# A convolution chain's last stage: resident rows loaded ahead of the raw coefficients, and scaled five pieces later

## The chip, the cores and the metric

The kernel runs on one core of a Trainium2 chip. The metric is the device time of one launch in microseconds (us). Before the change three runs took 2479.8, 2480.79 and 2481.91 us; the median is 2480.79.

## The reference

Four layers are applied in turn to x of shape (4, 64, 256, 256), all in float32:

```python
def conv(x, ...):                      # layers 0, 2 and 3
    k = einsum('ijk,imk->ijmk', hx, hy)[0].transpose(2, 0, 1)  # rank-one filters from two small sine networks
    y = irfft2(rfft2(x, s=(512, 512)) * rfft2(k, s=(512, 512)) / 512, s=(512, 512))[..., :256, :256]
    return y + x * bias[:, None, None]
def haar(x, v, conv_w, tau):           # layer 1
    f1 = haar2d(x)                     # Haar transform of each image
    for i in range(2):
        f4 = einsum('bchw,oc->bohw', f1 * v[i], conv_w[i])
        acc += sign(f4) * relu(abs(f4) - tau[i])               # soft threshold
    return haar2d(acc, inverse=True) + x
x = conv(x, L0); x = haar(x, L1); x = conv(x, L2); x = conv(x, L3)
```

A filter is the product of a row filter and a column filter, so a convolution becomes matmuls with one triangular Toeplitz matrix for the rows and one for the columns. The multiplication by v commutes with the sum over channels, so the kernel applies it after the channel matmul.

## The kernel before, in words

The work is cut into 64 tiles t: two groups of two images, 32 rounds a group, four images of 256 x 256 to a tile (128 x 2048 floats). Phase A (`phase_a`) runs layer 0 and the forward transform, phase B (`phase_b`) mixes the channels and thresholds, phase C (`phase_c`) makes the inverse transform and layers 2 and 3. Phases pass data through DRAM tensors: `coef` (A to B), `mixed` and `unshrunk` (B to C). For the second group, phase B leaves the threshold of its second filter undone: it writes the raw coefficients to `unshrunk`, and phase C thresholds them. That is the step called `shrink`.

The order of the instructions is written out by hand: every engine runs its own list in the order in which the Python code emits it. A phase is a list of pieces. A round of phase C has 18 pieces, j = 0 to 17, in `piece(t, j)`. TensorE does in one round:

- j 0 to 3: rows of layer 2 for tile t (`c1r`), in two pairs of pieces
- j 4: first half of the inverse transform's matmul for tile t+1 (`c0ps`, L352)
- j 5 to 8: columns of layer 3 for tile t-2 (`c2c`)
- j 9 to 12: rows of layer 3 for tile t-1 (`c2r`)
- j 13: second half of `c0ps`
- j 14 to 17: columns of layer 2 for tile t (`c1c`)

Each pair of pieces, and each half of `c0ps`, takes one pair of PSUM banks from `banks()`, ten pairs a round. Three pairs of banks are used in turn, so a new one can be written only when the pair asked for three places earlier has been copied out. Copies out are put off with `later()` and emitted by `flush()` at the start of the next piece: ScalarE copies `c1r` and `c2r` to `ch` (L913) and `c0ps` to `z` (L901); VectorE adds the bias term to `c2c` and `c1c` (L932, to `o` and `cy`).

Beside this, GpSimd does the inverse transform's additions along the rows (L429) two tiles ahead, after ScalarE has scaled the loaded tile `g` (L406, seven multiplications). From round 29 on (t = `alone` - `AHEAD` = 32 - 3), shrink works three tiles ahead, for tile 32 and later. For each half of a tile it has five operations: x = raw * v into PSUM (VectorE, L845), its sign (ScalarE, L847), its absolute value (ScalarE, L849), minus the threshold (VectorE, L851), and the last product (VectorE, L854). GpSimd then adds the result to `g` (L880). `SHRINK` holds the pieces in which these ten operations are emitted. Both v and the threshold come from one resident tile `rows`, loaded once (L821, two DMAs of 512 KB) from `in_v_rows` and scaled in place by `scale_rows` with 14 ScalarE multiplications (L406).

All DMAs are issued by SyncE (SP). Eight semaphores are used in turn for them, so a DMA is issued only after the one eight places earlier has landed. A `raw` tile takes four DMAs of 256 KB (L816), a `g` tile four of 256 KB (L810), a Toeplitz pair four of 112 KB (L163), a `mixed` or `unshrunk` store one of 512 KB (L721, L729). The SBUF pool `late`, which holds `rows`, `raw` and `shrunk`, is opened where phase B's pool is closed, just ahead of round 29. In that round the emission is: j 0 loads raw 32, then rows; j 1 loads g 32; j 2 loads the filters of tile 30, and `scale_rows`; j 3 to 17 shrink 32, shifted by two pieces; j 5 loads raw 33.

Of the kernel before, what the change touches and what calls it, by code (L numbers as in the profile page):

```python
# [51 lines left out]
BLOCKS = N // ROW  # L52
# [28 lines left out]
C_PIECES = 4 * BLOCKS + 2  # L81
AHEAD = 3
SHRINK = (1, 2, 3, 5, 6, 10, 11, 12, 14, 15)
W = 2 * N

PAIR = 2 * 2 * ROUNDS * NB * W + NB * W

# [13 lines left out]
def conv_haar_kernel(  # L101
# [10 lines left out]
    def coefficients(name):  # L112
        return dram.tile([CI, STEPS // 2, PAIR], F32, tag=name, name=name)
# [3 lines left out]
    unshrunk = coefficients("unshrunk")  # L117
    thresholds = dram.tile([STEPS, 2, SHARED, 2 * W + PAD], F32, tag="thresholds", name="thresholds")
    filt = [dram.tile([ROUNDS, 2, REPEATS, ITEMS, PERIOD], F32, tag=f"filt{l}", name=f"filt{l}") for l in range(NL)]
# [176 lines left out]
    def half(r):  # L296
        return slice(r * ROW, (r + 1) * ROW)
# [13 lines left out]

    tau_sb = mp.tile([P, 2, W], F32, tag="tau", name="tau_sb")
    per_level_sb = mp.tile([P, N], F32, tag="per_level", name="per_level_sb")
# [11 lines left out]
    def put_thresholds(copies):  # L325

        n = copies.stop - copies.start
        of = tau_sb.rearrange("p i w -> p (i w)").unsqueeze(1).to_broadcast([P, n, 2 * W])
        nc.sync.dma_start(thresholds.rearrange("s r c w -> (s r) c w")[:, copies, : 2 * W], of)

# [111 lines left out]
    def flush():  # L442
        ops = list(waiting)
        waiting.clear()
        for op in ops:
            op()
# [5 lines left out]
    def all_rows(grp_tile, r, images, joined):  # L452

        parts = images.rearrange("(m q) (h n) k -> q m h (n k)", q=2, h=2)
        n = NB * W
        pairs = []
        for q in range(2):
            for h in (slice(0, 2),) if joined else (slice(0, 1), slice(1, 2)):
                at = grp_tile.offset + ((h.start * 2 + q) * ROUNDS + r) * n
                rows = [[PAIR, P // 2], [2 * ROUNDS * n, h.stop - h.start], [1, n]]  # L460
                pairs.append((bass.AP(grp_tile.tensor, at, rows), parts[q][:, h]))
        return pairs
# [329 lines left out]
    def phase_c():  # L792
# [7 lines left out]
        def load(t, k=slice(0, 4)):  # L800
            if t >= total:
                return
            if t < 2:
                g = bp.tile([P, 2, 2, W], F32, tag="v", name=f"g_{t}", bufs=3)
                st[t]["g"] = g.rearrange("p i k w -> p (i k w)").rearrange("p (n k) -> p n k", k=N)
            elif k.start == 0:
                st[t]["g"] = big("in", f"g_{t}", 3)
                st[t]["scales"] = scales(st[t]["g"])
            for rows, g in all_rows(mixed[t // ROUNDS], t % ROUNDS, st[t]["g"], False)[k]:
                nc.sync.dma_start(g, rows)  # L810

        def load_raw(t):
            if alone <= t < total:
                r = st[t]["raw"] = late["sb"].tile([P, 2 * M, N], F32, tag="raw", name=f"raw_{t}", bufs=2)
                for rows, to in all_rows(unshrunk, t % ROUNDS, r, False):
                    nc.sync.dma_start(to, rows)  # L816

        def load_rows():
            late["rows"] = late["sb"].tile([P, 2, 2, W], F32, tag="rows", name="rows")
            for r in range(2):  # L820
                nc.sync.dma_start(late["rows"][half(r)].rearrange("p k s w -> p (k s w)"), v_rows)  # L821

        def scale_rows():
            for k in range(2):
                for op in scales(late["rows"][:, k].rearrange("p s (h k) -> p (s h) k", h=2), (1.0, 0.5)[k]):
                    pass

        def shrink(t, k):

            if not alone <= t < total:  # L830
                return
            s = st[t]

            def split(name, h):
                return s[name].rearrange("p (s b h) k -> p s b (h k)", s=2, b=NB)[:, h]

            def rows(k, h):
                return late["rows"][:, k, h].unsqueeze(1).to_broadcast([P, NB, W])

            h, op = divmod(SHRINK.index(k), 5) if k in SHRINK else (0, -1)  # L840
            if op == 0:
                if h == 0:
                    s["shrunk"] = late["sb"].tile([P, 2 * M, N], F32, tag="shrunk", name=f"shrunk_{t}", bufs=2)
                s["x"] = late["ps"].tile([P, NB, W], F32, tag="x", name=f"x_{t}_{h}")
                nc.vector.tensor_tensor(s["x"], split("raw", h), rows(0, h), ALU.mult)  # L845
            elif op == 1:
                nc.scalar.activation(split("shrunk", h), s["x"], AF.Sign)  # L847
            elif op == 2:
                nc.scalar.activation(s["x"], s["x"], AF.Abs)  # L849
            elif op == 3:  # L850
                nc.vector.tensor_tensor(s["x"], s["x"], rows(1, h), ALU.subtract)  # L851
            elif op == 4:
                to = split("shrunk", h)
                nc.vector.scalar_tensor_tensor(to, s["x"], 0.0, to, ALU.max, ALU.mult)  # L854

        def scaled(t, count):
            if count and 1 < t < total:
                run(st[t]["scales"], count)

        def filters(t, l):  # L860
            if t < total:
                st[t]["toep", l] = load_toeplitz(l, t)
# [11 lines left out]
        def sums(t):  # L874
            if t < total:
                s = st[t]
                if t >= alone:
                    for h in range(2):
                        to, of = (s[k].rearrange("p (s n) k -> p s (n k)", s=2)[:, h] for k in ("g", "shrunk"))
                        nc.gpsimd.tensor_tensor(to, to, of, ALU.add)  # L880
                s["ci"] = big("t1", f"ci_{t}", 2)
                s["ops"] = inverse_free(s["g"], s["ci"], f"i{t}_", nc.vector if t < 2 else nc.gpsimd, levels(t))
# [54 lines left out]
        def store(t):  # L937
            if t < total - 1:
                n = 2 * CI if t < alone else CI
                for k in range(0, 2 * M, n):  # L940
                    stores.append(lambda k=k, y=st[t]["y"]: nc.sync.dma_start(out[t // ROUNDS, t % ROUNDS][:, k : k + n], y[:, k : k + n]))
            st[t].clear()
            for put in stores[: len(stores) if t >= alone else 1]:
                put()
            del stores[: len(stores) if t >= alone else 1]
# [3 lines left out]
        def piece(t, j):  # L949
            flush()  # L950
            if j == 0:
                sums(t + 2)
            if t >= alone - AHEAD:
                if j == 1:
                    load(t + 3)
            elif t == 0:
                pass
            elif j in (1, 3, 5, 7):
                load(t + 3, slice(j // 2, j // 2 + 1))
            if stores and j == C2 + BLOCKS + 3:  # L960
                stores.pop(0)()
            if j == 2:
                filters(t + 1, 1)
            if j == C2 + BLOCKS + 1 and t > 1:
                store(t - 2)
            if j == R2 + BLOCKS:
                filters(t, 2)
            first = t == alone - AHEAD
            if t >= alone - AHEAD:
                if j == 0 and first:  # L970
                    load_raw(alone)
                    load_rows()
                if j == 2 and first:
                    scale_rows()
                if j == BLOCKS + 1:
                    load_raw(t + AHEAD + 1)
                shrink(t + AHEAD, j - 2 * first)
            if R1 <= j < R1 + BLOCKS:
                if t < total:
                    rows(t, 1, j - R1)  # L980
            elif C2 <= j < C2 + BLOCKS:
                if 1 < t:
                    columns(t - 2, 2, j - C2)
            elif R2 <= j < R2 + BLOCKS:
                if 0 < t <= total:
                    rows(t - 1, 2, j - R2)
            elif j >= C1:
                if t < total:
                    columns(t, 1, j - C1)
            else:  # L990
                product(t + 1, int(j > BLOCKS))
            if t == 0:
                scaled(3, 2 * (2 * BLOCKS <= j < C1))
                scaled(2, int(j > 0))
            else:
                scaled(t + 3, {11: 3, 12: 2, 15: 1, 16: 1}.get(j, 0))
            if j > 0:
                step(t + 2, 1)
# [183 lines left out]
```

## Time and profile before

The profiled execution took 2491.59 us, of which its span is 2489.8 us; the median of the unprofiled runs is 2480.79 us.

| what | value |
|---|---|
| TensorE busy | 2261.5 us, 91% of the span |
| GpSimd busy | 2055.6 us, 83% |
| VectorE busy | 1792.3 us, 72% |
| ScalarE busy | 1392.0 us, 56% |
| moved by DMA | 688.03 MB, mean 276 GB/s |
| mean granted TensorE clock | 0.983 |

A profile's times are those of one execution, in us from the start of its span. "Busy" is the time in which an engine worked on an instruction; DMA issues and waits are not counted. A wait is named after what ended it. Rounds 29 and later begin near 1787 us and run to the end.

### The profile page before, as it was taken

The numbers are of one execution on the slowest core, as the hardware profiler recorded it, in microseconds if no ns is written. First come the engines' busy times: TensorE is split into PE (matmuls) and PEld (weight loads), VectorE is DVE, ScalarE is ACT, GpSimd is POOL, SyncE is SP. The second block draws the span as 40 slices with busy tenths as digits, with TensorE's granted clock in tenths as the row PEclk, the third lists the DMA queues.
The fourth block names the chain that finished last, engine by engine and source line by source line (L and its number), as shares of the span: only waits on it lengthen the run. The fifth ranks groups of instructions, "written<-read, shape, count | busy, mean of one in ns | idle before, by whom it ended". The sixth has DMA issues, their size and how long they took to land.

```text
span 2489.8 us, 119298 instructions
## 1 busy us (share of the span) xinstructions
PE 2261.5 (91%) x53298; PEld 1874.7 (75%) x53298; DVE 1792.3 (72%) x1959; ACT 1392.0 (56%) x2318; POOL 2055.6 (83%) x2412
## 2 busy tenths in 40 slices
PE   7999999777777777778999999999899999999999
PEld 5779897444444454556787887888789999999998
DVE  4533334999999999768777777777577777777763
ACT  2232233677777777255666666666555655565552
POOL 2988887899999999777777778777879999999990
PEclk9999999999999999888999999999999999999999
DMA  6778888899999999557999999999866666666643
GB/s 198 246 274 299 292 287 307 276 355 349 358 338 364 353 344 337 208 197 280 313 319 327 326 324 328 330 327 328 272 202 215 208 221 215 218 213 217 218 161 109
DMA packets 222969, 688.03 MB, mean 276 GB/s; under 512 B 31470, under 2 KB 32815, under 8 KB 218232
## 3 DMA queue, kind: packets, MB, share of 16 engines
q1 hardware_dynamic: 222456, 680.40, 78.5%
q8 instruction: 419, 6.86, 1.1%
q14 instruction: 94, 0.77, 0.1%
HBM read 428.16 MB, written 252.12 MB: 273 GB/s over the span
## 4 chain that ended last, share of the span: by engine, by line
PE 46%; DMA 4%; DVE 3%; issue 2%; SPq 1%; ACT 1%; DVEq 0%; ACTq 0%
PE c2r L340 10%; PE c2c L340 10%; PE c1c L340 9%; PE c1r L340 9%; PE c0ps L352 4%; PE f L653 3%; DMA g<-mixed 2%; DVE x L692 1%; DVE cy L932 1%; DMA toep<-filt 1%; SPq L163 1%; DVE x L672 0%; DMA raw<-in_v 0%; DMA unshrunk<-raw 0%; DVE m L697 0%
## 5 line engine op out<-in xcount | busy, mean ns | idle before, releaser
L429 POOL TENSOR_TENSOR i<-i,g 128x16 f32<-128x16 f32 x744 | 436.0, 606 | 27.2
L653 PE MATMUL f<-ft,mix 64*64 64x512 f32 x2048 | 304.2, 614 | 123.8 <-DVE x L672 108.0
L340 PEld LDWEIGHTS a2ps<-toep,ay 64*64 64x64 f32 x8192 | 303.6, 136 | 117.6 <-DVE f L521 52.7
L340 PE MATMUL a2ps<-toep,ay 64*64 64x192 f32 (+3 forms) x8192 | 337.1, 303 | 24.8 <-DVE f L521 20.5
L340 PEld LDWEIGHTS c2c<-toep,ch 64*64 64x64 f32 x8192 | 305.9, 135 | 55.5 <-ACT ch L913 14.8
L340 PEld LDWEIGHTS c1c<-toep,ch 64*64 64x64 f32 x8192 | 310.8, 133 | 42.6 <-issue 13.9
L340 PEld LDWEIGHTS a1ps<-toep,x 64*64 64x64 f32 x8192 | 285.5, 134 | 62.5 <-issue 39.3
L340 PE MATMUL c2c<-toep,ch 64*64 64x128 f32 (+3 forms) x8192 | 317.1, 299 | 11.9 <-ACT ch L913 10.0
L340 PE MATMUL c2r<-toep,cy 64*64 64x256 f32 (+3 forms) x8192 | 319.7, 298 | 5.1 <-issue 3.8
L340 PE MATMUL a1ps<-toep,x 64*64 64x256 f32 (+3 forms) x8192 | 315.4, 298 | 9.2 <-issue 5.3
L340 PEld LDWEIGHTS c2r<-toep,cy 64*64 64x64 f32 x8192 | 299.2, 134 | 32.2 <-issue 16.9
L340 PE MATMUL c1c<-toep,ch 64*64 64x128 f32 (+3 forms) x8192 | 317.6, 297 | 5.9 <-issue 4.9
L340 PE MATMUL c1r<-toep,z 64*64 64x256 f32 (+3 forms) x8192 | 314.5, 297 | 5.7 <-issue 3.7
L429 POOL TENSOR_TENSOR ci<-i,g 128x1024 f32<-128x1024 f32 x124 | 314.1, 2553 | 4.5
L340 PEld LDWEIGHTS c1r<-toep,z 64*64 64x64 f32 x8192 | 296.0, 133 | 28.7 <-issue 10.4
L715 POOL TENSOR_TENSOR gt<-m,ft 128x512 f32<-128x512 f32 x128 | 164.5, 1285 | 170.1 <-DVE m L697 150.9
L678 ACT ACTIVATE m<-x 128x1024 f32<-128x1024 f32 x194 | 205.9, 1061 | 165.8 <-DVE x L672 128.9
L488 ACT COPY ay<-a1ps 128x512 f32<-128x512 f32 x256 | 137.4, 589 | 275.7 <-PE a1ps L340 275.1
L913 ACT COPY ch<-c2r 128x512 f32<-128x512 f32 x256 | 137.4, 590 | 262.1 <-PE c2r L340 261.7
L672 DVE TENSOR_TENSOR x<-f,v 128x1024 f32<-128x1024 f32 x192 | 233.4, 1216 | 28.2 <-PE f L653 26.0
L508 DVE SCALAR_TENSOR_TENSOR x<-x,bias_sb,a2ps 128x512 f32<-128x512 f32 x256 | 179.5, 743 | 96.4 <-POOL f L390 48.4
L913 ACT COPY ch<-c1r 128x512 f32<-128x512 f32 x256 | 137.5, 594 | 164.5 <-PE c1r L340 164.1
(86 smaller groups left out, 3989.8 us busy)
## 6 DMA issues: line engine op xcount, KB each, us to landing
toep<-filt SPq DMA_DIRECT2D x768, 112.0 KB
ft<-coef SPq DMA_DIRECT2D x128, 512.0 KB
mixed<-gt SPq DMA_DIRECT2D x128, 512.0 KB
g<-mixed SPq DMA_DIRECT2D x256, 256.0 KB
x<-in_x SPq DMA_DIRECT2D x128, 256.0 KB
coef<-f SPq DMA_DIRECT2D x128, 256.0 KB
x<-in_x SPq DMA_DIRECT2D x32, 1024.0 KB
v<-in_v SPq DMA_DIRECT2D x64, 512.0 KB
```

Source lines behind the costliest of these rows:

```text
L163: nc.sync.dma_start(both[at : at + ROW // 2], src)
L340: nc.tensor.matmul(ps[r][half(c), j % 2, k * ROW :], data[half(r), c, k, bass.ts(j, ROW)], t(r, c)[:, : N - k * ROW], start=k == 0, stop=k ...
L352: nc.tensor.matmul(ps[r][half(c)].rearrange("p h k -> p (h k)"), matrix[half(r)], pairs(r, c).rearrange("p h k -> p (h k)"), start=True, s ...
L429: engine.tensor_tensor(to, s, d, op)
L488: later(lambda y=y, ps=ps: nc.scalar.copy(y, ps))
L508: nc.vector.scalar_tensor_tensor(to, old, bias_sb[:, c : c + 1], ps, ALU.mult, ALU.add)
L653: nc.tensor.matmul(un[u]["f4"][half(q), b, :], mixers[0][half(r), bass.ts(i, C)], st[s]["f"][half(r), b], start=True, stop=True, tile_posi ...
L672: nc.vector.tensor_tensor(un[u]["x"], un[u]["f4"], both(u, "v"), ALU.mult)
L678: nc.scalar.activation(un[u]["m"], un[u]["x"], AF.Sign)
L692: nc.vector.tensor_tensor(un[u]["a"], un[u]["a"], both(u, "tau"), ALU.subtract)
L715: nc.gpsimd.tensor_tensor(g[:, 0], m[:, 0], st[s]["f"][:, 0], ALU.add)
L913: later(lambda y=y, ps=ps: nc.scalar.copy(y, ps))
```

## The change

Only round 29 is touched, and in later rounds nothing of the emission. Rows are loaded at j 0 in place of raw 32; raw 32 at j 3; `scale_rows` is emitted at j 7, not 2; raw 33 at j 9, not 5; and shrink of tile 32 takes the ten pieces 8 to 17 in place of 3, 4, 5, 7, 8, 12, 13, 14, 16, 17. The arithmetic and the number of instructions are unchanged. Nothing in the diff touches phase B's parting step, which is on VectorE in both kernels.

```diff
 SHRINK = (1, 2, 3, 5, 6, 10, 11, 12, 14, 15)
+SHRINK_FIRST = (8, 9, 10, 11, 12, 13, 14, 15, 16, 17)
...
-        def shrink(t, k):
+        def shrink(t, k, order):
...
-            h, op = divmod(SHRINK.index(k), 5) if k in SHRINK else (0, -1)
+            h, op = divmod(order.index(k), 5) if k in order else (0, -1)
...
                 if j == 0 and first:
+                    load_rows()
+                if j == 3 and first:
                     load_raw(alone)
-                    load_rows()
-                if j == 2 and first:
+                if j == 7 and first:
                     scale_rows()
-                if j == BLOCKS + 1:
+                if j == (2 * BLOCKS + 1 if first else BLOCKS + 1):
                     load_raw(t + AHEAD + 1)
-                shrink(t + AHEAD, j - 2 * first)
+                shrink(t + AHEAD, j, SHRINK_FIRST if first else SHRINK)
```

## The prediction

> **What bounds the kernel now.** I first asked the page for its chain, then the busy times cut by rounds of phase C (a round begins with its first `c1r` matmul), then each engine's timeline around the one round that is long. Columns of the second fence: stretch, its length, busy time and instructions of PE, PEld, DVE, ACT and POOL, granted clock, DMA share, GB/s.
>
> ```profile
> PE 46%; DMA 4%; DVE 3%; issue 2%; SPq 1%; ACT 1%; DVEq 0%; ACTq 0%
> ```
>
> ```profile
> 1787.04:1817.46 30.42, 21.90 (x534) 19.13 (x530) 11.91 (x13) 14.95 (x37) 14.94 (x18) 0.83 0.76 227
> 1817.46:1838.40 20.94, 19.85 (x539) 18.35 (x534) 16.10 (x16) 12.45 (x24) 18.00 (x18) 1.00 0.61 200
> 1838.40:1858.00 19.60, 19.60 (x542) 18.18 (x537) 15.10 (x17) 11.61 (x22) 18.36 (x19) 1.00 0.67 217
> 1858.00:1877.19 19.19, 19.19 (x522) 15.73 (x516) 14.78 (x16) 10.86 (x21) 17.71 (x18) 1.00 0.65 214
> ```
>
> A settled round takes 19.19 us with PE busy throughout. Round 29 takes 30.42, 11.23 more; round 30 1.75 more; round 31 0.41 more. So 13.4 us is all that repairing round 29's neighbourhood can give. The timelines say why (start, length, engine, line; in brackets idle time and its end). PE, ACT, DVE, then POOL and SP:
>
> ```profile
> 1792.27 2.37 PE L340 MATMUL c2c<-toep,ch 64*64 64x256 f32 x64
> 1803.15 4.58 PE L340 MATMUL c2c<-toep,ch 64*64 64x256 f32 x58 [8.52 <-ACT ch L913]
> 1826.36 2.66 PE L340 MATMUL c2c<-toep,ch 64*64 64x256 f32 x58 [1.09 <-ACT ch L913]
> ```
>
> ```profile
> 1799.47 3.16 ACT L406 ACTIVATE rows<-rows 128x8 f32<-128x8 f32 x14 [8.96 <-DMA rows<-in_v_rows]
> 1802.54 1.04 ACT L913 COPY ch<-c1r 128x512 f32<-128x512 f32 x2
> ```
>
> ```profile
> 1801.14 2.48 DVE L845 TENSOR_TENSOR x<-raw,rows 128x1024 f32<-128x1024 f32 x1 [12.48 <-ACT rows L406]
> 1816.98 1.23 DVE L851 TENSOR_TENSOR x<-x,rows 128x1024 f32<-128x1024 f32 x1
> 1820.69 3.13 DVE L845 TENSOR_TENSOR x<-raw,rows 128x1024 f32<-128x1024 f32 x1
> ```
>
> ```profile
> 1797.87 4.66 POOL L429 TENSOR_TENSOR ci<-i,g 128x1024 f32<-128x1024 f32 x2
> 1818.05 4.68 POOL L880 TENSOR_TENSOR g<-g,shrunk 128x1024 f32<-128x1024 f32 x2 [15.52 <-DMA g<-mixed]
> ```
>
> ```profile
> 1784.36 0.58 SPq L721 DMA_DIRECT2D mixed<-gt  x1
> 1785.04 2.95 SPq L816 DMA_DIRECT2D raw<-unshrunk  x4
> 1788.04 1.74 SPq L821 DMA_DIRECT2D rows<-in_v_rows  x2
> 1789.82 3.00 SPq L810 DMA_DIRECT2D g<-mixed  x4
> 1792.92 7.04 SPq L163 DMA_DIRECT2D toep<-filt  x4
> 1800.22 3.22 SPq L816 DMA_DIRECT2D raw<-unshrunk  x4
> ```
>
> The second copy pair of `c1r` stands behind `scale_rows` on ACT, and that waits for rows, which lie behind raw 32 in the DMA queue. The second pair of `c2c` needs these banks (three places earlier in the rotation), so PE stops at 1794.63 for 8.52 us. The next two pieces then take 4.32 us (1803.15 to 1807.47) for a usual 2.18, and `c2r` 4.77 for 4.36: 2.55 lost to a halved clock. 8.52 + 2.55 is 11.1 of the 11.23.
>
> [...] granted 0.50 from 1798.03 to 1808.27. [...] the 12.48 and 8.96 us waits hold all behind them. [...] rows' second DMA, issued at 1789.18, landed at 1799.29, after raw. [...] L845, 1.23 us alone, took 2.48 and 3.13 by waiting for the end of a GpSimd instruction (1802.53; 1822.73) and then 1.09.
>
> **The change part by part.**
>
> *Scaling to j 7.* On ACT, the 14 scalings now stand after both `c1r` copies and the first `c0ps` copies. This takes the 8.52 us stop and its slow clock away. Cover: ACT has nothing but `sign` behind them until `c2r` is copied. Rows go first, right after mixed (landed 1788.87). Before, they took 5.14 us from raw's last landing (1794.15) to their own; so they land near 1794.0, at the latest 1796.1 (before's 1799.29 less raw's 3.2 us of transfer). Scaled 3.07 us later: 1797.1 to 1799.4, earlier than raw, as follows. Cost on the path: 0.
>
> *Raw 32 to j 3.* Its four DMAs pass rows, g 32 and toep 30 in SP's queue. The new order (mixed, rows, g, toep, raw) is the old one up to raw 33 with raw 32 taken out in front. So raw 33's landings of before are the template: its third DMA landed at 1806.79 (landings are the last of the events that a DMA's semaphore has in the trace). The first half's L845 waits for the first and third DMA alone in the built program. Raw 32's own transfer is 1.05 MB; the stretch 1788 to 1791 moved 325 GB/s: 3.2 us. Bounds: 2.6 at 401 GB/s, the fastest 5 us around; 5.3 from landing to landing (1788.87 to 1794.15). I take 3.2, since the DMA engines were busy all along (DMA share 0.89 to 1.04 from 1785 to 1800): the third DMA lands at **1803.6** (1801.5 to 1804.2), and L845 starts 0.15 later (rows to ACT took 0.18): 1803.75. POOL is idle from 1802.53, so it takes 1.23: it ends at E = **1804.98**. [...] g 32 moves up and is not needed early. g's second DMA waits on SP for the mixed store's landing (1788.87), behind 5 us of rows: 0. Toep 30 is needed in round 30: 0.
>
> *Who waits for L845.* Without a stop PE reaches j 13 (second `c0ps`) at 1792.27 + 2 x 4.36 = 1801.0. Behind L845 on DVE stand the two `o` additions of the second `c2c` pair, whose banks that `c0ps` takes. On ACT `sign` and `abs` wait for L845, and behind them stand the `c2r` copies, whose banks `c1c` takes. With the spacings of the same instructions in before:
>
> - DVE: `o` E+0.7, so `c0ps` starts E+0.7: **PE stops from 1801.0 to 1805.7, 4.7 us**.
> - ACT: sign E, abs E+0.95, `c2r` copies E+1.95, five g scalings E+2.9, `c2r` E+4.1, `z` E+5.0, second sign E+6.0, second abs E+6.9, two g scalings E+7.85 to 9.45.
> - PE: `c1c` E+2.5, its second pair E+4.7, round 30 starts E+6.9, and is at its second `c2c` pair, 7.41 later, at E+14.3 at the earliest.
> - POOL: L880, waiting for those scalings, E+9.5; its first instruction ends (2.36) E+11.9.
> - DVE: second L851 1.07 after the abs start, E+8.0; from it 3.71 to raw 33's L845 (1816.98 to 1820.69): E+11.7.
>
> This L845 arrives 0.2 us before the first L880 ends; [...] ends at E+13.0. In before it came 0.28 too late and lost 2. From its end to PE's resumption (sign, abs, first copy) before took 2.54 (1823.82 to 1826.36): **E+15.5 = 1820.5**. If it misses, it ends at E+15.3 and PE resumes at E+17.9 = 1822.9.
>
> *Sum.* In before PE resumed at this same matmul at 1826.36, and all after it is PE-bound and unchanged. Gain 1826.36 - 1820.5 = 5.9 us of the profiled 2491.59; its span is 9 us longer than the median, but the stretch is PE's and the queue's, so I take 5.9 off 2480.8: **2474.9**. Raw 33 moved to j 9 lands some 3 us after raw 32 and is wanted at E+11.7: 0.
>
> **The rivals.**
>
> *Slot missed or slow clock.* The 0.2 us margin is small. [...] Gain 3.5 to 4.5: about **2476.8**. For it: every spacing moves by tenths.
>
> *Clean.* Raw lands before 1798 and nothing takes the stop's place: up to 13.4, at least 10: **2468**. Against: it must pass 2 MB in the queue in 9 us, rows at 176 to 225 GB/s.
>
> *Slower: the queue stays slow.* Rows' stretch moved 176 GB/s (1791 to 1794). If g and raw run at that rate behind rows, rows and g, 2.1 MB, take 11.9 us after 1788.87, and g lands 2 us later, at 1802.8; only then do its semaphores let raw be issued. Raw's 5.0 us from issue to landing at 325 GB/s become 9.3: 1812.1. E is 1813.5; with a missed slot PE resumes at 1831.4: 5.0 slower, **2485.8**. It decides from a landing of 1809.5 on (1807.1 with the missed slot); each us later costs one. Against: after rows, g and raw 33 ran at 246 to 289.
>
> *The wait isn't removed:* rows land after 1800.7, so that ACT's scaling sets E. Rows would need 12 us for 1 MB from an earlier start; small, and then about 2477.
>
> **How the numbers follow.** As forecast 0.40; slot missed or slow clock 0.37; clean 0.10; raw up to 6 us late or rows late, within 0.2%, 0.07; slower rival 0.06, nearly all of it past the bound. A measurement tells about 0.2%, 5 us, from no change, so faster is above 5.0 us gained: 0.85 of the first case, a fifth of the second, all of the third: 0.51. Slower: 0.05. Same, the rest: 0.44. Range: from raw at 1801.5 (gain 8.0 and run spread) to a missed slot with raw at 1804.2 and 1 us more: 2472.3 to 2479.5, leaving out clean and the late cases, 0.2.
>
> **What would show it.** Right: no ACT wait for rows ahead of `ch` L913; the 8.52 gone; a wait of L845 for DMA raw ending near 1803.8; PE idle 4 to 5 us ahead of `c0ps` L352, not `c2c`; round 29 near 24.8 us, round 30 near 20.3; raw 33's L845 at 1.3 us. Wrong: no PE idle in round 29, or one over 10 us; L845 released by ACT rows; raw landing outside 1801 to 1805; any round from 32 on other than 19.2.

## The result and the profile after

The changed kernel took 2473.7 us (median of 20 runs) and the kernel before 2480.1 us (median of 20 runs beside it), so the medians are 6.4 us apart. The ratio was measured as 0.998, with a 95% interval of 0.997 to 0.9989, which is a gain of 5.0 us (2.7 to 7.4). The forecast was 2474.9 us, a gain of 5.9. The profiled execution of the changed kernel took 2475.71 us, with a span of 2473.9. That is 15.9 us below the profiled span of before, but 12.5 us of this lie ahead of round 29, where both kernels are the same. They are the spread between two executions, so the stages are compared from the start of round 29: 1787.04 before, 1774.57 after. Positions with a plus sign count from there. Lines behind `SHRINK_FIRST` (line 84) have moved down by one.

The page's chain of waits can't show the change, which is 6 us in 2474, a quarter of one per cent:

```profile
PE 46%; DVE 4%; DMA 2%; ACT 2%; issue 1%; SPq 1%; DVEq 0%; ACTq 0%
```

"DMA" has gone from 4% to 2% and VectorE from 3% to 4%, but one per cent is 25 us, so this tells of other stages of the two executions. Much more is seen in the busy times of rounds 29, 30 and 31 (columns as in the prediction):

```profile
1774.57:1799.42 24.85, 21.58 (x541) 18.30 (x536) 10.35 (x12) 13.43 (x35) 15.17 (x18) 1.00 0.87 264
1799.42:1820.24 20.82, 20.53 (x539) 18.86 (x534) 15.68 (x16) 13.97 (x26) 18.06 (x18) 1.00 0.70 224
1820.24:1839.44 19.20, 19.20 (x538) 18.40 (x534) 15.24 (x17) 11.83 (x22) 18.09 (x19) 1.00 0.64 217
```

Round 29 takes 24.85 us in place of 30.42, and the granted clock stays at 1.00. It is still 5.7 us longer than a settled round. TensorE's timeline of the changed kernel shows where (start, length, engine, line; in brackets the idle time and what ended it):

```profile
1778.82 1.47 PE L341 MATMUL c1r<-toep,z 64*64 64x128 f32 x40 [0.66 <-issue]
...
1785.91 1.68 PE L341 MATMUL c2c<-toep,ch 64*64 64x192 f32 x47 [1.85 <-issue]
...
1791.15 1.96 PE L341 MATMUL c2r<-toep,cy 64*64 64x192 f32 x51 [0.66 <-issue]
1792.95 1.73 PE L353 MATMUL c0ps<-ci,inverse_sb 64*64 64x512 f32 x8
...
1807.56 2.66 PE L341 MATMUL c2c<-toep,ch 64*64 64x256 f32 x58 [0.29 <-ACT ch L914]
```

The 8.52 us stop inside `c2c` is gone. In its place are three stops that end with "issue": TensorE waited for nothing that the semaphores show. The last line is the matmul at which the forecast measured its gain, the second pair of `c2c` in round 30: +32.99 (1807.56 less 1774.57), against +39.32 before (1826.36 less 1787.04). The gain there is 6.33 us.

ScalarE's and VectorE's timelines of the changed kernel:

```profile
1783.12 3.16 ACT L407 ACTIVATE rows<-rows 128x8 f32<-128x8 f32 x14 [0.77 <-DMA rows<-in_v_rows]
```

```profile
1791.02 1.23 DVE L846 TENSOR_TENSOR x<-raw,rows 128x1024 f32<-128x1024 f32 x1 [6.26 <-DMA raw<-unshrunk]
1792.16 1.40 DVE L933 SCALAR_TENSOR_TENSOR o<-cy,bias_sb,c2c 128x512 f32<-128x512 f32 x2
...
1803.75 1.27 DVE L846 TENSOR_TENSOR x<-raw,rows 128x1024 f32<-128x1024 f32 x1
```

The scaling of the rows waits 0.77 us, not 8.96. The first step of tile 32 now waits for raw 32, not for the rows, and ends at 1792.25 (+17.68). Tile 33's step takes 1.27 us, not 3.13. GpSimd's and SyncE's timelines of the changed kernel:

```profile
1801.55 5.67 POOL L881 TENSOR_TENSOR g<-g,shrunk 128x1024 f32<-128x1024 f32 x2 [11.26 <-ACT g L407]
```

```profile
1772.73 1.56 SPq L822 DMA_DIRECT2D rows<-in_v_rows  x2
1774.35 4.10 SPq L811 DMA_DIRECT2D g<-mixed  x4
1778.55 5.13 SPq L164 DMA_DIRECT2D toep<-filt  x4
1783.72 6.41 SPq L817 DMA_DIRECT2D raw<-unshrunk  x8
```

The order in the queue is the one forecast. The two `g` additions of GpSimd, 4.68 us before, take 5.67: the first ends at 1803.93, and the second takes 3.35 us, where it took 2.36, while tile 33's step runs (1803.75 to 1805.02). That step ends 1.09 us after the first addition. The trace of before has this throughout: 63 of the 64 multiplications of L845 end 1.08 to 1.10 us after a GpSimd instruction has ended, and the one that ran with GpSimd idle took 1.23 us. In the changed kernel 62 of the 64 do so, and the two others took 1.23 us.

**What the "issue" stops are.** The trace records a 16,384-byte packet of kind "instruction" for TensorE's queue every 4.5 us (median of rounds 33 to 60), 419 in the whole execution. That they are blocks of TensorE's instructions is read from their number: TensorE has 107,270 instructions in the trace, 256 for each packet. The packets of round 29 in the changed kernel, with the stops beside them:

```
packet begins  took   ends      TensorE goes on   later by
1776.48        0.95   1777.43   1778.82           1.39
1783.48        1.07   1784.55   1785.91           1.36
1788.40        1.35   1789.75   1791.15           1.40
```

All three stops end 1.36 to 1.40 us after a packet has landed. The places of the stops fit this too. With TensorE's instructions numbered from 0 in order of time, and cut into blocks of 256, all 28 stops of over 0.25 us that end with "issue" in the trace of before end at number 193 or 194 of a block, and so do 14 of the 15 in the changed kernel.

That gives two theories of what holds round 29 after the change. *Raw*: the wait for raw 32 that the forecast named sets the end. *Instructions*: while the rows are moved, TensorE's instructions come late. The experiments below take the two apart. The intervals of the measured ratios are some 0.1% (2.5 us) to each side, so they seldom separate two changed versions; for that the traces are used, one execution of each.

### The profile page after: what moved, and what is told of

The parts are those of the page before. It is cut to its first block, busy times and chain, and to the rows that moved or that the text cites. A ratio compares the mean times of both kernels' runs of the same rounds, so it can differ in the third digit from the quotient of the medians.

```text
span 2473.9 us, 119298 instructions
## 1 busy us (share of the span) xinstructions
PE 2260.7 (91%) x53298; PEld 1883.8 (76%) x53298; DVE 1791.3 (72%) x1959; ACT 1392.7 (56%) x2318; POOL 2066.2 (84%) x2412
## 4 chain that ended last, share of the span: by engine, by line
PE 46%; DVE 4%; DMA 2%; ACT 2%; issue 1%; SPq 1%; DVEq 0%; ACTq 0%
PE c2c L341 10%; PE c2r L341 10%; PE c1c L341 10%; PE c1r L341 9%; PE c0ps L353 4%; PE f L654 4%; DMA g<-mixed 1%; DVE x L693 1%; DVE cy L933 1%; DVE m L698 1%; DMA toep<-filt 1%; DVE x L673 1%; DMA rows<-in_v_rows 0%; ACT ch L914 0%; DVE o L933 0%
## 5 line engine op out<-in xcount | busy, mean ns | idle before, releaser
L430 POOL TENSOR_TENSOR i<-i,g 128x16 f32<-128x16 f32 x744 | 442.8, 616 | 27.2
L341 PE MATMUL a2ps<-toep,ay 64*64 64x128 f32 (+3 forms) x8192 | 336.9, 303 | 24.0 <-DVE f L522 20.6
L341 PEld LDWEIGHTS c1c<-toep,ch 64*64 64x64 f32 x8192 | 315.8, 133 | 42.9 <-issue 10.5
L341 PEld LDWEIGHTS c2c<-toep,ch 64*64 64x64 f32 x8192 | 306.5, 133 | 42.8 <-issue 12.5
L341 PE MATMUL c1c<-toep,ch 64*64 64x256 f32 (+3 forms) x8192 | 323.0, 297 | 5.5 <-ACT ch L914 3.3
L341 PE MATMUL a1ps<-toep,x 64*64 64x128 f32 (+3 forms) x8192 | 314.2, 298 | 5.7 <-DMA toep<-filt 2.4
L341 PE MATMUL c2c<-toep,ch 64*64 64x256 f32 (+3 forms) x8192 | 315.7, 297 | 3.0 <-issue 2.6
```

Of the source, the lines that this page charges most:

```text
L341: nc.tensor.matmul(ps[r][half(c), j % 2, k * ROW :], data[half(r), c, k, bass.ts(j, ROW)], t(r, c)[:, : N - k * ROW], start=k == 0, stop=k ...
L430: engine.tensor_tensor(to, s, d, op)
```

## The experiments

| kernel | median, us | ratio to before (95%) | round 29, us | second `c2c` of round 30 |
|---|---|---|---|---|
| before | | 1 | 30.42 | +39.3 |
| changed | 2473.7 | 0.998 (0.997 to 0.9989) | 24.85 | +33.0 |
| late_scale | 2474.6 | 0.9979 (0.9967 to 0.9991) | 25.42 | +34.2 |
| rows_first | 2478.98 | 0.9992 (0.9978 to 1.0006) | 30.09 | +39.0 |
| rows_raw_first | 2474.44 | 0.9979 (0.9967 to 0.9991) | 25.36 | +33.3 |
| no_raw | 2473.14 | 0.9969 (0.9955 to 0.9983) | 25.39 | +34.2 |
| rows_4k | 2473.52 | 0.9979 (0.9968 to 0.999) | 26.50 | +35.4 |
| rows_padded | 2474.41 | 0.9985 (0.9969 to 1.0) | 24.98 | +33.1 |
| no_rows | 2471.08 | 0.9964 (0.9944 to 0.9984) | 25.12 | +32.7 |
| split_rows | 2472.4 | 0.9968 (0.9956 to 0.9981) | 24.27 | +31.8 |
| early_v | 2470.86 | 0.9971 (0.9962 to 0.9981) | 20.50 | +29.7 |
| early_v_paced | 2471.54 | 0.9976 (0.9964 to 0.9989) | 22.08 | +29.7 |
| no_loads | 2468.44 | 0.9954 (0.9936 to 0.9972) | 19.18 | +27.3 |
| extra_load | 2576.44 | 1.0399 (1.0376 to 1.0422) | 26.49 | +34.1 |

The medians of before beside them were 2479.49 (first four experiments), 2479.4 (next four) and 2477.59 us (last four). All diffs are against the changed kernel.

extra_load differs from the changed kernel from round 33 on only, so its round 29 is a second execution of the changed one. It took 26.49 us where the other took 24.85, and the last column differs by 1.1 us. Differences of that size between two rows of the last two columns tell nothing.

### One half of the change at a time: late_scale and rows_first

late_scale keeps the later scaling and puts the loads back in their old order:

```diff
                 if j == 0 and first:
-                    load_rows()
-                if j == 3 and first:
                     load_raw(alone)
+                    load_rows()
```

> Only the later scaling and shrink of round 29; the loads keep their old order (raw 32, rows, g 32 at j 0 and 1). Times from the start of round 29; PE's return to the second c2c pair of round 30 is at 39.3 us in the kernel before and 33.0 in the changed one. Theory (the later scaling is the whole gain, and whichever of rows and raw is second in the queue sets L845): rows land near 12.3, their first half is scaled at 14.1, L845 waits for ACT and ends near 16.6 [...], so PE returns at 31.9: 7.4 us faster than before, 1 us better than the full change. Rival (asking for rows first is needed): L845 is at 17 or later and PE returns at 35 or later, a gain of 4 us or less.

rows_first keeps the new order of the loads and scales early, as before:

```diff
-                if j == 7 and first:
+                if j == 2 and first:
                     scale_rows()
...
-                shrink(t + AHEAD, j, SHRINK_FIRST if first else SHRINK)
+                shrink(t + AHEAD, j - 2 * first, SHRINK)
```

> Only the order of the loads (rows, g 32, filters, raw 32, raw 33 at j 9); scaling back at j 2 and shrink in its old pieces. Theory (the order alone trades one wait for another): rows land near 8.4 from the start of round 29, the c1r copies end near 12.7, PE stops at the second c2c pair from 7.4 to 12.3; then L845 and sign wait for raw until 16.4 and hold the z copies on ACT, so PE stops again, before c2r, until about 19. Round 29 takes 28 to 31 us, PE's return in round 30 is at 36 or later: 2 to 4 us faster than before. Rival (the order is what removes the stop): round 29 within 1 us of the changed kernel's 24.85.

The later scaling alone gives the same ratio as the whole change; that the new order of the loads adds anything to it isn't shown. TensorE's timeline of late_scale, in round 29 and in round 30:

```profile
1787.65 2.46 PE L341 MATMUL c2c<-toep,ch 64*64 64x192 f32 x47 [2.40 <-issue]
...
1809.34 2.66 PE L341 MATMUL c2c<-toep,ch 64*64 64x256 f32 x58 [0.27 <-ACT ch L914]
```

The 8.52 us stop is gone here too. VectorE's first step waits for the scaled rows and ends at +15.9, earlier than the theory's 16.6, but TensorE is back at +34.2, not at +31.9: instruction stops of 1.53 and 2.40 us and 3.4 us at half clock, which the theory left out, came first. The trace gains 5.1 us on before. The new order alone gives 0.5 us, which is not told from nothing. TensorE's timeline of rows_first shows why:

```profile
1793.15 4.25 PE L341 MATMUL c2c<-toep,ch 64*64 64x256 f32 x64 [2.54 <-ACT ch L914]
1798.70 7.61 PE L341 MATMUL c2r<-toep,cy 64*64 64x256 f32 x122 [1.30 <-DVE o L933]
```

The stop behind the scaling shrinks from 8.52 to 2.54 us and ends at +11.9, not +16.1, since the rows land earlier. But raw 32 now lands later, VectorE's first step waits 13.66 us for it with the `o` additions behind it, and TensorE waits for those. The clock was at 0.5 for 10.2 us, so that the `c2r` matmuls took 7.61 us, where 4.55 is usual. The wait was moved from one tile to the other. In the whole change the scaling and the shrink steps are late enough for both.

### Raw's wait taken away: rows_raw_first and no_raw

rows_raw_first asks for raw 32 right behind the rows, ahead of `g` 32 and the filters:

```diff
                     load_rows()
-                if j == 3 and first:
                     load_raw(alone)
```

> As the changed kernel, but raw 32 is asked for right after rows, ahead of g 32 and the filters. Theory (raw's landing sets L845, and after it the chain of 15.3 us up to PE's return): raw's third DMA lands near 11.5 from the start of round 29 instead of 16.3, L845 starts there or when the running ci instruction of GpSimd ends (13.4), ends at 12.7 to 14.5, PE returns in round 30 at 28 to 30 unless late instruction pages hold it: 9 to 11 us faster than before, round 29 near 21. Rival (PE's waits for instruction pages, 4.4 us in the changed kernel's round 29, are the bound): round 29 stays near 24 and the gain at 6 to 7 us.

no_raw doesn't load raw 32 at all:

```diff
                 r = st[t]["raw"] = late["sb"].tile([P, 2 * M, N], F32, tag="raw", name=f"raw_{t}", bufs=2)
+                if t == alone:
+                    nc.vector.memset(r, 0.0)
+                    return
```

> As the changed kernel, but tile 32's raw coefficients are not loaded: the tile is set to zero on VectorE, so tile 32's second threshold term is left out. Theory: without the wait for raw, L845 starts when rows are scaled, near 10.2 from the start of round 29, and PE returns in round 30 at its own pace, 26.6 to 28: 11 to 12.5 us faster than before. Rival (rows' wait or instruction pages bound it as well): PE returns at 31 or later, a gain under 8.5 us.

Round 29 stays at 25.4 us in both, so raw's wait alone isn't what keeps it long. In rows_raw_first the first step ran at +10.9, well before it is needed, and one stop of 3.22 us appeared inside `c2c`. TensorE's timeline of no_raw has the same at another place:

```profile
1782.11 2.71 PE L341 MATMUL c1r<-toep,z 64*64 64x128 f32 x40 [3.18 <-issue]
```

It ends 1.43 us after an instruction packet. These 40 matmuls, 1.47 us in the changed kernel, take 2.71 here, because the clock was at 0.5 for 6.8 us around them, 5.7 of it behind the stop; at half speed that costs 2.9 (an estimate, half of 5.7). Stop and clock are 6.1 us together, about the 6.2 that the round is too long. In the changed kernel the instruction stops came as three of at most 1.85 us, and the clock did not fall.

### The size of the rows' packets: rows_4k and rows_padded

In the changed kernel the rows' packets of 8192 bytes took 584 ns (median), and those of 4096 bytes in raw's transfer 159. I suspected the large packets.

```diff
-            for r in range(2):
-                nc.sync.dma_start(late["rows"][half(r)].rearrange("p k s w -> p (k s w)"), v_rows)
+            for k in range(2):
+                for r in range(2):
+                    nc.sync.dma_start(late["rows"][half(r), k].rearrange("p s w -> p (s w)"), v_rows[:, k])
```

> Edit: the rows are asked for in four loads of 4096 bytes a partition in place of two of 8192 bytes; the order and the scaling stay as in the changed kernel. Positions count from the start of round 29. Theory (the 8192-byte packets, some 620 ns each where 4096-byte ones take 160 to 200, hold the DMA engines and with them the packets that bring TensorE's instructions): the rows land near +6.5 in place of +8.45, TensorE's issue gaps in round 29 fall from 3.2 us to under 1.5, raw 32 is complete near +14.5, round 29 is 22 to 23 us, TensorE is back on its way in round 30 near +30, and the gain over the kernel before is 8 to 9 us. Rival (any full queue delays the instruction packets, whatever the size of its packets): rows near +8.4, gaps of 3 us or more, round 29 near 25, TensorE back near +33, a gain near 6.

rows_padded keeps two loads, but with spare floats behind each 4096 bytes in DRAM:

```diff
-                nc.sync.dma_start(late["rows"][half(r)].rearrange("p k s w -> p (k s w)"), v_rows)
+                nc.sync.dma_start(late["rows"][half(r)].rearrange("p k s w -> p k (s w)"), v_rows[:, :, : 2 * W])
...
-        "v_rows": f(np.stack([by_block("v"), by_block("tau")], axis=1)),
+        "v_rows": padded(np.stack([by_block("v"), by_block("tau")], axis=1)),
```

> Edit: the rows lie in DRAM with 128 spare floats behind each half, so that the two loads move 4096-byte pieces at a pitch of 4608 bytes; two loads as in the changed kernel. Theory: as with four loads of 4096 bytes (rows near +6.5, round 29 22 to 23 us, a gain of 8 to 9), and if the pitch of a power of two is part of the 620 ns, rows before +6 and a gain of 9 to 10. Rival: rows near +8.4, round 29 near 25, a gain near 6.

The theory fell. The rows landed at +9.0 and +7.75, not at +6.5, and round 29 was no shorter. The rival's instruction stops of 3 us or more did not come either: those of over 0.25 us are 0.87 us in rows_4k and 2.61 in rows_padded. There TensorE stopped ahead of `c0ps` instead, for `o` and so for raw 32, by 2.87 and 0.86 us. TensorE's timeline of rows_4k:

```profile
1785.37 1.73 PE L353 MATMUL c0ps<-ci,inverse_sb 64*64 64x512 f32 x8 [2.87 <-DVE o L934]
```

In rows_4k 256 KB of rows landed every 0.9 to 1.3 us, where a 256 KB part of raw landed every 0.64. So the rows are slow to move whatever the size or pitch of their packets. Why stays open. Neither 8192 bytes nor a kernel input as the source is enough: the other 4,197 packets of 8192 bytes in the changed kernel's trace, nearly all of them of the kernel input x, took 309 ns (median). That both loads of the rows read the same 512 KB was not tried apart.

### The rows taken away: no_rows, and both: no_loads

```diff
-            for r in range(2):
-                nc.sync.dma_start(late["rows"][half(r)].rearrange("p k s w -> p (k s w)"), v_rows)
+            nc.vector.memset(late["rows"], 0.0)
```

> Edit: the rows are not loaded but set to zero on VectorE at the place where they were asked for, so that the values and thresholds of the last stage's tiles from 32 on are left out of the result. Theory (the rows' packets are what holds the queue): raw 32 lands before +11, no issue gap of TensorE over 1 us in round 29, round 29 19.2 to 21 us, TensorE back in round 30 at +27 to +29, a gain of 11 to 12 us. Rival (raw's and the 512 KB of g alone fill the queue enough to starve TensorE of instructions): a gap of 1.5 us or more remains, round 29 is 23 or more, gain 7 or less.

Half of the theory held: the instruction stops of over 0.25 us are gone from round 29. The round is still 25.12 us. VectorE's and TensorE's timelines of no_rows:

```profile
1789.03 3.39 DVE L845 TENSOR_TENSOR x<-raw,rows 128x1024 f32<-128x1024 f32 x1 [4.18 <-DMA raw<-unshrunk]
```

```profile
1793.13 2.10 PE L353 MATMUL c0ps<-ci,inverse_sb 64*64 64x512 f32 x8 [2.41 <-DVE o L932]
```

With nothing to stop it earlier, TensorE is at `c0ps` sooner and there meets the very wait that the forecast named: raw 32's step, then `o`, then `c0ps`. The step itself takes 3.39 us, where it took 1.23 in the changed kernel. After the 2.41 us stop the clock fell for 3.4 us. no_loads has both edits, no_rows' and no_raw's:

> Edit: neither the rows nor raw 32 are loaded; both are set to zero on VectorE where they were asked for, so that the last stage's tiles from 32 on are left out of the result. It takes both limits away at once. Theory (two limits stand side by side in round 29, the late instructions of TensorE while the rows are moved and the late raw tile [...], and either alone keeps the round at 24 to 25 us): round 29 is 19.2 to 20.5 us, no issue gap of TensorE above 0.5 us in it, TensorE is at its second c2c pair of round 30 at +26.6 to +28, and the gain over the kernel before is 10 to 13 us. Rival (something else holds the round, the pool that changes at its start [...]): round 29 stays at 23 us or more, gain 7 or less.

Its round 29, by the busy times:

```profile
1775.79:1794.97 19.18, 19.18 (x540) 15.77 (x536) 15.12 (x15) 14.12 (x36) 15.22 (x18) 1.00 0.68 228
```

That is a settled round to 0.01 us. So the two loads are the whole of round 29's excess, as far as one execution of each kernel tells. Raw 32's wait and the late instructions stand side by side, and either of them alone keeps the round at 25 us: without raw 25.39, without rows 25.12, with both 24.85, with neither 19.18.

### What a load costs TensorE by itself: extra_load

```diff
+                if j == 0 and alone - AHEAD + 4 <= t < total - 2:
+                    more = late["sb"].tile([P, 2, 2, W], F32, tag="more", name=f"more_{t}", bufs=1)
+                    for r in range(2):
+                        nc.sync.dma_start(more[half(r)].rearrange("p k s w -> p (k s w)"), v_rows)
```

> Edit: in each round from 33 to 61 the rows are loaded once more, 1 MB in two loads at piece 0, into a tile that nothing reads; everything else is the changed kernel. It measures by itself what such a load costs TensorE through its instructions, 29 times. Theory: each of these rounds shows issue gaps of TensorE that end 1.1 to 1.6 us after a 16384-byte instruction packet, 1 to 3 us a round, so the rounds are 20.2 to 22.2 us in place of 19.2, and the kernel is 30 to 85 us slower than the changed one. Rival (a load that nobody waits for costs nothing, and round 29 was late for its waits alone): rounds of 19.2 to 19.4 us and a time within 6 us of the changed kernel's. If waits of GpSimd or VectorE for g or raw appear ahead of TensorE's stops, the test says little, and the waits are named.

The kernel became 103 us slower than the changed one, more than the 30 to 85 expected. Two lines of its TensorE timeline, then three of its waits in rounds 33 to 60:

```profile
1883.05 0.34 PE L341 MATMUL c1r<-toep,z 64*64 64x64 f32 x6 [2.49 <-issue]
...
1907.18 1.06 PE L341 MATMUL c1r<-toep,z 64*64 64x192 f32 x24 [2.46 <-issue]
```

```profile
PE c1r L341 <- issue: 44.7, 19, 3.3
...
PE c2c L341 <- issue: 10.6, 7, 2.1
...
PE c1c L341 <- ACT ch L914: 4.2, 9, 0.7
```

The columns of the second fence are the sum, the number and the longest. Rounds 33 to 60 took 645.4 us, against 539.7 in the changed kernel: 3.8 us a round for one megabyte that nobody reads. TensorE had 39 stops of over 0.25 us in them, 63.0 us in sum; 31 of these, 59.2 us, ended 1.1 to 1.6 us after an instruction packet. In the changed kernel's same rounds there is one such stop, of 0.5 us. A stop's idle time is counted from the end of the matmul before it. Counted from that matmul's start to the next one's, the 39 stops are 74.6 us. The clock was at 0.5 in twelve stretches of 3.4 us, which costs up to another 20.5 (12 times half of 3.41). The other 11 us or so are not accounted for. TensorE's matmuls waited under 6 us in sum for other engines or for raw, so they are not it.

The DMA share of these rounds is 0.76, against 0.64 in the changed kernel. The engines were far from full in the mean. When TensorE asks for a block isn't recorded; only its landing is. So it is shown that the rows' transfer makes blocks late, and not on what they wait.

### Fewer bytes or another place: split_rows, early_v and early_v_paced

split_rows asks for the half with the values, then raw 32, then the half with the thresholds, in loads of 4096 bytes a partition:

```diff
                 if j == 0 and first:
-                    load_rows()
-                if j == 3 and first:
+                    load_rows(0)
                     load_raw(alone)
+                    load_rows(1)
```

> Edit: the half of the rows that holds the values is asked for at piece 3 ahead of raw 32, the half that holds the thresholds at piece 4 behind it, both in loads of 4096 bytes a partition. Theory: raw 32 lands near +11 and does not stop VectorE's first step of tile 32, TensorE's gaps in round 29 stay under 1.5 us, round 29 is 20 to 22 us, TensorE is back in round 30 near +28 to +30, and the gain is 9 to 11 us. Rival (the same bytes keep the same engines full, and TensorE's instructions late): gaps of 3 us or more, round 29 near 25, a gain near 6.

The kernel that ran asks for all three at piece 0; the piece numbers in the expectation are a slip. Raw 32 landed at +6.2 (its third load) and its step ran at +10.2 without a wait, but instruction stops of 0.98, 1.58 and 1.32 us remained and round 29 took 24.27 us: the rival's side. The clock did not fall.

early_v moves half of the rows out of the round:

```diff
+            if t == 20 and j == 4:
+                load_rows(0)
+            if t == 21 and j == 8:
+                scale_rows(0)
...
                 if j == 0 and first:
-                    load_rows()
-                if j == 3 and first:
                     load_raw(alone)
-                if j == 7 and first:
-                    scale_rows()
+                    load_rows(1)
+                if j == 9 and first:
+                    scale_rows(1)
```

> Edit: the half of the rows with the values lives in a tile of its own, loaded in round 20 and scaled in round 21; in round 29 raw 32 is asked for at piece 0, the threshold half (512 KB in two loads) behind it, and the thresholds are scaled at piece 9. Theory: half the extra bytes, so TensorE's instruction gaps in round 29 fall from 3.2 to 1 to 2 us, raw 32 lands near +5 and stops nobody, round 29 is 21 to 23 us, TensorE is back in round 30 near +29 to +30, gain 9 to 11 us. Rival (the place in round 29 is full whatever is taken out): round 29 at 24 or more, gain near 6.

In early_v_paced the threshold half is asked for at piece 5 (`if j == 5 and first: load_rows(1)`):

> Edit: as with the values loaded in round 20, and in round 29 the threshold half is asked for at piece 5, behind g 32 and the filters of tile 30, in place of piece 0. Theory: the same bytes in fewer places at once; instruction gaps in round 29 under 1 us, the threshold half lands near +12, before its scaling is reached near +11 to +13, round 29 is 20 to 22 us, gain 10 to 12 us. Rival: no difference from asking for it at piece 0[...].

TensorE's timeline of early_v:

```profile
1784.72 1.68 PE L341 MATMUL c2c<-toep,ch 64*64 64x192 f32 x47 [0.48 <-issue]
...
1804.95 1.29 PE L341 MATMUL c2c<-toep,ch 64*64 64x256 f32 x18 [1.33 <-ACT ch L913]
```

early_v's round 29 is 20.50 us, with this one instruction stop of over 0.25 us; its theory had 21 to 23 us. In early_v_paced one of 1.75 us came back and the round took 22.08: asking later did not help. Both are at the second `c2c` of round 30 at +29.7, because early_v loses 1.3 us there to tile 33's step, which took 3.39 us, and early_v_paced's took 1.26. Their traces are 3.3 us ahead of the changed kernel's. By the medians they are 6 to 7 us faster than before, as the changed kernel is, so that they beat it is not shown.

## Why the forecast was right, step by step

- **The scaling at j 7 frees the path: right.** The rows landed at +8.45 (forecast +7.0 to +9.1) and were scaled by +11.7 (+10.1 to +12.4), and ScalarE's wait fell from 8.96 to 0.77 us. late_scale, which has this step alone, has the same ratio; its trace keeps 5.1 of the 6.3 us.
- **Raw 32 becomes the new wait: right.** Its third load landed at +16.3 (+16.6), the step ended at E = +17.68 (+17.94), and `c0ps` started 0.70 us after it (0.7). The chain behind it came as laid out: `c1c` at E + 2.5 (2.5), round 30 at E + 7.2 (6.9), GpSimd's additions at E + 9.3 (9.5), tile 33's step at E + 11.5 (11.7).
- **"PE stops from 1801.0 to 1805.7, 4.7 us", ahead of `c0ps`: wrong as a picture, right as a sum.** TensorE was not idle for 4.7 us there. Measured against no_loads, whose round is settled, it was 1.1 us late at the start of `c2c`, 3.2 at `c2r`, 4.4 at `c0ps` and 5.4 at `c1c`. The three instruction stops are 3.2 us of idle time; counted from start to start of the matmuls around them, they are nearly all of the 4.4. So TensorE came to `c0ps` just as the first `o` ended. The last 1.0 us is what raw's step cost it by itself: the second bank of `c0ps` waited for the second `o`, and `c1c` for ScalarE's copies behind the sign and the absolute value. The forecast put late instructions at nothing: it worked with settled matmul times in a stretch whose DMA load is not settled. That cost nothing in the sum, since raw's step would have held `c0ps` until then in any case. That the two limits met so closely is chance: in extra_load, whose round 29 has the same emission, and in rows_4k, TensorE came earlier and made the forecast stop, for 2.43 and 2.87 us, and `c0ps` started 0.71 us after E in both. TensorE's timeline of extra_load:

```profile
1787.92 2.63 PE L353 MATMUL c0ps<-ci,inverse_sb 64*64 64x512 f32 x8 [2.43 <-DVE o L933]
```

- **A slow clock, named among the rivals: it did not come in the profiled execution**, whose idle time was cut into stops of at most 1.85 us. It came in extra_load's round 29 (behind the stop of 2.43 us), in no_raw (3.18), rows_raw_first (3.22), rows_4k (2.87), late_scale (2.40) and no_rows (2.41). All of these are shorter than the stop of 4.7 us that was forecast. What the slow clock adds to the 0.37 was the author's estimate.
- **The slot behind GpSimd's first addition: right.** Tile 33's step took 1.27 us. The margin was as thin as was said: in seven of the eleven experiments other than extra_load this step took 3.0 to 3.4 us. A missed slot costs what was forecast. Where the slot was met behind the same order of loads, in the changed kernel, rows_padded and extra_load, the second `c2c` of round 30 came at E + 15.3 to 15.5; in rows_4k and no_raw, where it was missed, at E + 17.6 and 17.8 (forecast 17.9). TensorE's stop there is only 1.1 us, because in both it had lost time to a slow clock before.
- **Round 29 at 24.8: 24.85. Round 30 at 20.3 to 20.4: 20.82.** The second pair of `c2c` came at E + 15.3 (15.5). Some 0.65 us were then lost inside `c1c` of round 30, without a stop over 0.25 us; what took them stays open.
- **"Unchanged after": the emission is, the times are not.** Rounds 32, 33, 39, 40 and 49 were 19.4 to 20.0 us in this one execution, 2.8 us in sum; this was one of the forecast's signs of being wrong. An instruction stop of 0.52 us in round 39 is part of it, the rest stays open. From the second `c2c` of round 30 to the end the trace of before took 663.4 us and that of the changed kernel 666.4; those of the other kernels but extra_load, with the same emission there, took 662.4 to 666.4. So the 6.33 us of the repaired stretch are 3.4 at the end of these two traces.
- **The gain: 5.9 forecast, 6.33 in the trace up to round 30, 6.4 between the medians, 5.0 by the ratio.** So close a meeting is in part luck: extra_load's execution of the same emission gives 5.2 up to round 30, and the interval of 2.7 to 7.4 holds the 3.5 of a missed slot too. The *clean* rival (10 to 13.4 us) needed raw before 1798; no_loads shows that with neither load the trace gains 12.0 up to round 30. The *slower* rival needed raw at 1809.5, at +22.5 of before's round; it was complete at +17.0.

## What to carry to other kernels

Moving a consumer behind the work that others wait for gave the gain here (4.9 us by the medians of late_scale and before), while changing the order of the loads alone (0.5 us in rows_first) only passed the wait from one tile to the next; ask of each order what stands behind the operation that will now wait. When a stop of TensorE ends with "issue" in a stretch with heavy loads, look for the instruction packets before you look for a semaphore, and price an added load by what it does to them too: in extra_load one megabyte a round cost 3.8 us. When taking a wait away gains nothing, take away the other suspect, and then both at once: here two limits of the same length hid each other (round 29 took 25.39 and 25.12 us with one of them gone, 19.18 with neither).

## What the hardware showed that was not expected

- TensorE's instructions come by DMA, 16,384 bytes every 4.5 us here, and are not always in time. Over the whole profiled execution 28 stops of TensorE over 0.25 us end with "issue" in the kernel before (23.2 us in sum), and 27 of them end 1.1 to 1.6 us after such a packet. In the changed kernel they are 15 (13.3 us), 13 of them so; in rows_4k 15 (10.2 us), 13 of them so. By chance a tenth would fall in that window, as it is 0.5 us of some 4.8. These stops vary between executions of the same stages, and so are a candidate for the spread of 10 to 20 us between the runs of one kernel; that was not tested.
- One megabyte of the rows, loaded once a round for nobody, cost TensorE 3.8 us a round at a mean DMA share of 0.76, while early_v's round 29, at 0.93, is 1.3 us longer than a settled one, with one stop of 0.48. The share does not say whether instructions come late.
- Half clock came here with stops as short as 2.12 us. In the fourteen traces, from round 29 on, each of the ten stops of 2.67 us or more has a stretch at half clock that starts in it or up to 2.1 us behind it, and so have ten of the fourteen between 2.0 and 2.66 us, the shortest of them 2.12 us. None below starts one; the longest of them is 1.92 us.
